# Two attention blocks on one core: weight stores and raw loads pinned in the transfer queue, normalising steps and chores at other places

## The chip, the cores and the metric

The kernel runs on one core of one Trainium2 chip. The metric is the device time in microseconds (us) of one execution; the number given for a kernel is the median of its runs. The core has five engines with a queue of instructions each: TensorE (PE, matrix products), VectorE (DVE) and ScalarE (ACT) for elementwise work, GpSimd (POOL) and SyncE (SP). Here SP issues the transfers (DMA) of weights, images and small exchanges, and POOL issues those that add one tile to another in flight. [...]

## What is computed

Two self-attention blocks one after the other, on 8 images of 512 channels and 32 x 32 positions (1024 positions), all in float32. Each block normalises its input in 8 groups of channels, makes queries, keys and values, attends in 8 heads of 64 channels, projects, and adds its input. The second block is the same with other weights. Cut to one block:

```python
xg = x.reshape(B, GROUPS, -1)
xn = ((xg - mean) * rsqrt(var + EPS)).reshape(B, C, H, W) * gamma + beta
qkv = einsum('oc,bchw->bohw', qkv_w, xn) + qkv_b
q, k, v = (B, 8 heads, 64, 1024 positions) each
attn = softmax(einsum('bhds,bhdt->bhst', q, k) * 64 ** -0.5, axis=-1)
out = einsum('bhst,bhdt->bhds', attn, v).reshape(B, C, H, W)
return x + einsum('oc,bchw->bohw', proj_w, out) + proj_b
```

## The kernel before

**Jobs.** One image in one layer is a job. The 16 jobs run in the order (image 0, layer 0), (1, 0), (0, 1), (1, 1), then the same for the next pair of images. Each job has a projection phase for V, for the output O of the job before, and for K and Q, and then an attention. The two phases alternate: while the attention of job n runs on TensorE, the other engines prepare the projections of job n+1.

**Projections.** The products are done with the seven products of Strassen's scheme, nested twice in the "deep" form (lines 801 and 806). Each weight therefore needs seven sums of its blocks, which are made once on VectorE and kept in DRAM. `factor` (lines 162 to 168) does one of four steps of such sums. Three helpers feed it: `load_blocks` (line 157) loads the four raw blocks, `store_factors` writes the sums of one level to DRAM (`keep`), and `deep_round` loads four blocks into a tile `round`, does both levels of sums on it, and stores the seven results (`deep`, line 235). `ROUNDS` says that jobs 0 to 3 each make one such round, in their attention; `FIRST` says that jobs 0 and 1 also make first-level sums (tile `raw`) there, through `put_first`. `prepare` makes the second-level sums of a first-level weight in place and stores them (line 209) after a delay given to `later`. `fetch` loads weights in advance into slots of the pool that also holds the exponentials e. The inputs of the deep form are sums too, of the normalised image: `combine` (lines 423 to 429) and `inner_sums` (lines 482 to 488, tile `deep`). The SBUF tiles named raw, round and deep share one tag, so they follow one another in the same place.

**Attention.** 64 steps per job, 8 groups of 8. A step makes scores of one block of keys against half of the queries (line 1099), ScalarE takes the exponential (line 1104), TensorE multiplies by V two steps later (line 1150). The row sums of the exponentials are added up beside this: in most groups the first four blocks are added in pairs by POOL's transfers (line 1127) and then to `acc` by VectorE (line 1130), the rest directly by VectorE (lines 1118 and 1120). At the end of a group ScalarE copies half of the result to `px` (line 1171) and VectorE adds the other half (line 1173). `reduce` makes the row sums of a group (line 1185); for every second group a chain follows that crosses the DMA queue twice: `r` is gathered by three transfers (line 1208), VectorE inverts (lines 1212 to 1232), the result `rt` goes to DRAM as `rd` (line 1225), comes back spread over partitions as `rb` in two transfers (line 1227), and VectorE multiplies (line 1242). In jobs with a round the first inversions are put off by 12.0 and the multiplication by 22.0 in planned time.

**What sets the order.** The program counts its own planned time: `advance` moves it by 1.71 per attention step, and `later(delay, fn)` puts a piece of work at a planned time. Chores of an attention are put at step numbers in two tables, `chores` (`put`) and `moves` (`move`); both step to the next free number when the wanted one is taken. Thus a table holds at most one chore per step, but the two may hold one each. The order on PE, ACT, DVE and POOL is the order of the program text. SP's instructions are ordered by a scheduler instead, from an estimate of when their inputs are ready, unless one is marked to stay in its place in the program: this is what `tc.keep_in_program_order` does.

The chores of an attention of job n, as far as they matter here: the normalisation of the next image is `reads` (statistics) and `steps`: one for the group sums, one for the factors (lines 349 to 351), and four `apply`, one ScalarE pass each (line 356); then the four `combine`, and the eight `inner_sums`, which `deep_steps` returns with those from xn first (line 482 `deep<-xn` first) and those from t after.

Of the kernel before, what the change touches and what calls it, by code (L numbers as in the profile page):

```python
# [19 lines left out]
P = 128  # L20
# [21 lines left out]
FACTOR = {1: A11, 2: A12, 3: S4, 4: A22, 5: S1, 6: S2, 7: S3}  # L42
# [12 lines left out]
ROUNDS = {0: (O, 0), 1: (V, 1), 2: (O, 1), 3: (V, 0)}  # L55
# [26 lines left out]
def fast_path(  # L82
# [10 lines left out]
    nc = tc.nc  # L93
# [18 lines left out]
    xs = {}  # L112
# [3 lines left out]
    def later(delay, fn):  # L116
        todo.append((clock[0] + delay, fn))
# [25 lines left out]
    def raw_block(layer, which, i, j):  # L143

        if which == O:
            w, at = wp[layer], 0
        else:
            w, at = wqkv[layer], {Q: 0, K: C, V: 2 * C}[which]
        cols = slice(at + i * CH, at + (i + 1) * CH)
        return w[j * CH : (j + 1) * CH, cols].rearrange("(cc p) o -> p cc o", p=P)  # L150

    factors, deep, begins = {}, {}, []

    def load_blocks(w, layer, which):
        for i in range(2):
            for j in range(2):
                nc.sync.dma_start(w[:, 2 * j + i], raw_block(layer, which, i, j))

    def factor(w, part):

        if part == 0:
            nc.vector.tensor_add(w[:, S1], w[:, S3], w[:, A22])
        elif part == 1:
            nc.vector.tensor_sub(w[:, S2], w[:, S1], w[:, A11])
        elif part == 2:
            nc.vector.tensor_sub(w[:, S3], w[:, A11], w[:, S3])
        else:
            nc.vector.tensor_sub(w[:, S4], w[:, A12], w[:, S2])

    def store_factors(w, layer, which):  # L170
        keep = wdram.tile([P, NW, 2, CH], F32, name=f"keep_{which}_{layer}")
        for s in (slice(S1, NW), slice(S3, S3 + 1)):
            nc.sync.dma_start(keep[:, s], w[:, s])
        factors[which, layer] = keep

    plan, held, raw = deque(), {}, set()
# [22 lines left out]
    def prepare(key):  # L199
        if key not in raw:  # L200
            return False
        raw.discard(key)
        n, which, o = key
        w = held[key]
        for part in range(4):
            factor(w, part)
        keep = wdram.tile([P, NW, P], F32, name=f"deep_{which}_{jobs[n][1]}_{o}")
        deep[which, jobs[n][1], o] = keep
        later(1.0, lambda: nc.sync.dma_start(keep, w))
        return True  # L210

    def deep_round(which, layer):


        box = []

        def start():
            t = acts.tile([P, NW, NW, P], F32, tag="deep", name=f"round_{which}_{layer}")
            box.append(t)
            for i in range(2):  # L220
                for j in range(2):
                    nc.sync.dma_start(
                        t[:, 2 * j + i, 0:4, :].rearrange("p (cc h) o -> p cc (h o)", cc=2),
                        raw_block(layer, which, i, j),
                    )

        def outer_(part):
            factor(box[0][:, :, 0:4, :], part)

        def inner(part):  # L230
            factor(box[0].rearrange("p f a o -> p a f o"), part)

        def store(o):
            keep = wdram.tile([P, NW, P], F32, name=f"deep_{which}_{layer}_{o}")
            nc.sync.dma_start(keep, box[0][:, FACTOR[o]])
            deep[which, layer, o] = keep

        first = [lambda part=part: outer_(part) for part in range(4)]
        second = [lambda part=part: inner(part) for part in range(4)]
        return start, first, second, [lambda o=o: store(o) for o in OUTER]  # L240
# [8 lines left out]
    def x_tile(b):  # L249
        xs[b] = xpool.tile([P, NC, S], F32, tag="x", name=f"x_{b}")  # L250
        return xs[b]
# [5 lines left out]
    def load_steps(b):  # L257

        def chunk(cc):
            if cc == 0:  # L260
                x_tile(b)
            nc.sync.dma_start(xs[b][:, cc, :], x[b, cc * P : (cc + 1) * P, :])

        return [(15 + cc, lambda cc=cc: chunk(cc)) for cc in range(NC)]

    class Norm:
# [20 lines left out]
        def sums(self, cc):  # L287

            nc.scalar.activation(
                xn[0][:, cc, :], xs[self.b][:, cc, :], AF.Identity, accum_out=self.mv[:, cc, 0:1]  # L290
            )
# [108 lines left out]
    def norm_steps(n):  # L400
        norm = Norm(n)

        def place():
            xn[0] = acts.tile([P, NC, S], F32, tag="xn", name=f"xn_{n}")

        def factors():
            norm.factors(slice(0, NC))
            place()

        reads = [lambda cc=cc, sh=sh: norm.stat(cc, sh) for cc in range(NC) for sh in range(2)]  # L410
        reads.append(norm.gather)
        steps = [norm.groups, factors] + [lambda cc=cc: norm.apply(cc) for cc in range(NC)]
        return reads, steps
# [220 lines left out]
    def deep_phases(n, extra, outs=None, early=()):  # L634
# [340 lines left out]
        for which, o in chains[:2]:  # L975
            prepare((job(which), which, o))
# [20 lines left out]
    def last_weights(n):  # L997
        w = acts.tile([P, NW, 2, CH], F32, tag="deep", name="w_last")
        layer = jobs[n][1]
        load_blocks(w, layer, O)  # L1000
        return w
# [341 lines left out]
    def extend_plan(n):  # L1343
        plan.extend((n, V, o) for o in (OUTER_V if n >= DEEP_V else ORDER))
        plan.extend((n - 1, O, o) for o in (OUTER if n >= DEEP_V else ORDER))
        plan.extend((n, which, o) for which in (K, Q) for o in OUTER)
# [192 lines left out]
    reads, steps = norm_steps(1)  # L1539
    for n in range(-1, len(jobs)):  # L1540
        last = n + 1 == len(jobs)
        outs = None
        if n >= 0:
            chores, moves = {}, {}

            def put(i, fn):
                while i in chores:
                    i += 1
                chores[i] = fn
                return i  # L1550

            def move(i, fn):
                while i in moves:
                    i += 1
                moves[i] = fn
                return i
# [12 lines left out]
                    at = move(at + 1 + i % 2, fn)  # L1569

            def put_first(which, layer):
                at = move(31 if n == 0 else 3, lambda: start()) + 3
                box = []

                def start():
                    box.append(acts.tile([P, NW, 2, CH], F32, tag="deep", name=f"raw_{n}"))
                    load_blocks(box[0], layer, which)

                for part in range(4):
                    at = put(at + 1, lambda part=part: factor(box[0], part))  # L1580
                move(at + 1, lambda: store_factors(box[0], layer, which))

            if last:
                w = last_weights(n)
                for part in range(4):
                    put(12 + 2 * part, lambda part=part: factor(w, part))
                for i, fn in enumerate(last_sums(0)):
                    put(49 + 3 * i, fn)
            else:
                for i, (_, fn) in enumerate(extra):  # L1590
                    put(2 + i, fn)
                if n == 1:
                    at = (8, 14, 15, 16, 18, 19, 21, 24, 27, 30)
                else:
                    for i, fn in zip((3, 3, 4, 5, 5, 6, 7, 7, 8), reads):
                        put(i, fn)
                    at = (16, 22, 23, 24, 26, 27, 29, 31, 33, 35)
                    if n < DEEP_V + 2:
                        at = (17, 23, 24, 25, 27, 28, 30, 32, 34, 36)
                for i, fn in zip(at, steps):  # L1600
                    put(i, fn)
                if n == 1:
                    put_first(*FIRST[n])
                if n in ROUNDS:
                    put_round(*ROUNDS[n])
                if n == 0:
                    put_first(*FIRST[n])
                for i, fn in zip(at[len(steps) :], sums(n + 1)):
                    put(i, fn)
                put(52 if n in ROUNDS else 48, lambda q=att.q: out_combine(q, None, 0))  # L1610
                deep_first = deep_steps(n + 1)
                if n + 1 >= DEEP_V:
                    for i, fn in enumerate(deep_first):
                        put(37 + 2 * i if n not in ROUNDS else (39, 40, 41, 43, 45, 47, 49, 50)[i], fn)
                else:
                    for at, fn in zip((46, 47, 48, 49), deep_first[4:]):
                        put(at, fn)
                move(58, lambda: extend_plan(n + 1))
                for _ in range(RING):
                    move(58, fetch)  # L1620
            assert max([*chores, *moves], default=0) < NT * len(att.groups) + LEAD
            if n + 1 >= DEEP_V and not last:
# [10 lines left out]
                if n + 2 < len(jobs):  # L1633
                    reads, steps = norm_steps(n + 2)
# [34 lines left out]
            if n + 2 < len(jobs):  # L1669
                reads, steps = norm_steps(n + 2)  # L1670
# [264 lines left out]
```

## Time and profile before

| what | us |
|---|---|
| median of 3 runs | 3175.92 (3175.18 to 3176.13) |
| the profiled execution | 3175.27 |
| its span, first to last instruction | 3173.5 |
| mean granted TensorE clock | 0.998 |
| ACT busy: exponentials, 1024 of 1025 ns | 1043.5 |
| PE busy: scores and values, 8192 matmuls each | 1058.3 and 1057.6 |
| DVE busy: accumulation (L1118, L1120, L1130) | 156.4, 389.7, 272.6 |

The profile's page gives each engine's busy time, the span in 40 slices, the DMA queues, the chain of work that ended last, and the costliest groups of instructions. Other views of the same trace give the instructions in order of time with the idle time before each and what ended it, or the busy time in chosen windows. The profiled time is 1.8 us longer than the span, and 0.65 us below the median. The DMA issues that matter here, from the page (queue, operation, count, size, and the median time from issue to landing):

```profile
w<-deep SPq DMA_DIRECT2D x399, 448.0 KB, 5.3
e<-e POOLq DMA_DIRECT2D x224, 512.0 KB, 4.7
...
rb<-rd SPq DMA_DIRECT2D x96, 256.0 KB, 3.9
...
deep<-w SPq DMA_DIRECT2D x28, 448.0 KB, 2.7
deep<-round SPq DMA_DIRECT2D x28, 448.0 KB, 4.4
```

### The profile page before, as it was taken

How to read it: one execution, taken by the hardware profiler on the slowest of the kernel's cores; microseconds unless marked ns; L12 is line 12 of the kernel's file. 1: busy time of each engine (PE TensorE's matmuls, PEld its weight loads, DVE VectorE, ACT ScalarE, POOL GpSimd, SP SyncE). 2: the span in 40 equal slices, each digit the busy share in tenths (PEclk: the TensorE clock that was granted, in tenths of full speed). 3: DMA queues.
4: the chain of work that ended last, by engine and by line, in shares of the span. 5: the costliest groups of instructions: out<-in, count | busy, mean ns of one | idle time of the engine just before them, and what ended most of it. 6: DMA issues, size and time to landing. Idle time of an engine off the chain costs nothing.

```text
span 3173.5 us, 62149 instructions
## 1 busy us (share of the span) xinstructions
PE 3153.8 (99%) x24093; PEld 1875.1 (59%) x24093; DVE 2635.5 (83%) x3571; ACT 2330.9 (73%) x4233; POOL 280.9 (9%) x318
## 2 busy tenths in 40 slices
PE   9999999999999999999999999999999999999999
PEld 7356384663846639366483754837557375573844
DVE  8797898978879788796978969789697887978967
ACT  5648687786877768777686776867768687686864
POOL 0100101001010010101001000010000100001000
PEclk9999999999999999999999999999999999999999
DMA  8546675565735455455554535446456463445733
GB/s 277 142 129 167 159 211 136 142 188 142 229 75 147 110 132 146 82 163 148 145 179 93 161 92 144 120 95 186 129 137 182 89 198 66 132 126 95 223 75 82
DMA packets 186190, 450.31 MB, mean 142 GB/s; under 512 B 37928, under 2 KB 54176, under 8 KB 185888
## 3 DMA queue, kind: packets, MB, share of 16 engines
q1 hardware_dynamic: 137040, 296.82, 27.7%
q0 software_dynamic: 48848, 149.44, 25.9%
q8 instruction: 192, 3.15, 0.4%
q14 instruction: 110, 0.90, 0.1%
HBM read 247.41 MB, written 48.17 MB: 93 GB/s over the span
## 4 chain that ended last, share of the span: by engine, by line
PE 90%; DVE 5%; DMA 2%; issue 1%; SPq 0%; ACT 0%; DVEq 0%; POOL 0%; ACTq 0%; POOLq 0%
PE sc L1099 24%; PE po L1150 24%; PE vd L806 11%; PE zd L806 11%; PE yd L806 5%; PE ud L806 4%; PE vd L801 4%; PE zd L801 3%; DVE acc L1120 1%; PE ud L801 1%; PE yd L801 1%; DMA rb<-rd 1%; PE z L553 1%; DMA rd<-rt 1%; DVE acc L1130 1%
## 5 line engine op out<-in xcount | busy, mean ns | idle before, releaser
L1104 ACT ACTIVATE e<-sc 128x1024 f32<-128x1024 f32 x1024 | 1043.5, 1025 | 575.1 <-PE sc L1099 546.9
L1099 PE MATMUL sc<-q,k 64*64 64x512 f32 x8192 | 1058.3, 589 | 2.8 <-ACT e L1104 2.8
L1150 PE MATMUL po<-e,v 64*64 64x512 f32 x8192 | 1057.6, 589 | 1.9 <-ACT e L1104 1.9
L1150 PEld LDWEIGHTS po<-e,v 64*64 64x64 f32 x8192 | 313.1, 133 | 567.9 <-issue 541.9
L1099 PEld LDWEIGHTS sc<-q,k 64*64 64x64 f32 x8192 | 310.9, 133 | 566.6 <-issue 506.0
L1120 DVE TENSOR_TENSOR acc<-acc,e 128x1024 f32<-128x1024 f32 x320 | 389.7, 1218 | 37.9 <-ACT e L1104 27.1
L1127 POOL DMA_DIRECT2D e<-e x224 | 192.8, 861 | 1758.7 <-ACT e L1104 1302.8
L1118 DVE TENSOR_TENSOR acc<-e,e 128x1024 f32<-128x1024 f32 x128 | 156.4, 1222 | 145.8 <-ACT e L1104 145.8
L1130 DVE TENSOR_TENSOR acc<-acc,e 128x1024 f32<-128x1024 f32 x224 | 272.6, 1217 | 1.7
L806 PE MATMUL zd<-deep,w 128*128 128x256 f32 x860 | 240.2, 379 | 1.0 <-ACT ud L501 1.0
L806 PE MATMUL vd<-deep,w 128*128 128x256 f32 x804 | 223.5, 379 | 0.0
L806 PEld LDWEIGHTS zd<-deep,w 128*128 128x128 f32 x860 | 163.3, 190 | 23.6 <-ACT ud L501 1.4
L806 PEld LDWEIGHTS vd<-deep,w 128*128 128x128 f32 x804 | 152.8, 190 | 20.8
L1185 DVE TRANSPOSE_TENSOR_REDUCE r<-acc 128x32 f32<-128x1024 f32 x128 | 159.4, 1245 | 4.3
L901 POOL DMA_DIRECT2D x<-p x61 | 72.9, 1195 | 972.3 <-ACT p L823 379.0
L848 DVE TENSOR_TENSOR p<-p,s 128x512 f32<-128x512 f32 x185 | 127.4, 689 | 20.5 <-ACT p L823 17.1
L801 PE MATMUL vd<-w,deep 128*128 128x128 f32 x840 | 119.3, 275 | 3.1 <-ACT ud L501 3.1
L848 DVE TENSOR_TENSOR q<-q,s 128x512 f32<-128x512 f32 x64 | 44.2, 690 | 87.0 <-ACT q L825 45.1
L801 PEld LDWEIGHTS vd<-w,deep 128*128 128x128 f32 x840 | 106.1, 192 | 3.6 <-ACT ud L501 3.6
L801 PE MATMUL zd<-w,deep 128*128 128x128 f32 x728 | 106.5, 275 | 0.3 <-ACT ud L501 0.3
L806 PE MATMUL vd<-os,w 128*128 128x256 f32 x364 | 105.5, 379 | 0.0
L1242 DVE TENSOR_TENSOR q<-q,rb 128x1024 f32<-128x1024 f32 x64 | 77.4, 1209 | 29.9 <-DMA rb<-rd 29.2
(296 smaller groups left out, 4849.7 us busy)
## 6 DMA issues: line engine op xcount, KB each, us to landing
w<-deep SPq DMA_DIRECT2D x399, 448.0 KB, 5.3
e<-e POOLq DMA_DIRECT2D x224, 512.0 KB, 4.7
x<-p POOLq DMA_DIRECT2D x61, 512.0 KB, 6.4
rb<-rd SPq DMA_DIRECT2D x96, 256.0 KB, 3.9
x<-x_dram SPq DMA_DIRECT2D x28, 512.0 KB, 4.1
out_dram<-x SPq DMA_DIRECT2D x28, 512.0 KB, 5.0
deep<-w SPq DMA_DIRECT2D x28, 448.0 KB, 2.7
deep<-round SPq DMA_DIRECT2D x28, 448.0 KB, 4.4
```

What stands on the lines that cost most here:

```text
L801: nc.tensor.matmul(ps[:, tokens], moving[i][:, tokens], lhs[:, FACTOR[i], :], start=(start and ti == 0), stop=True, skip_group_check=True,)
L806: nc.tensor.matmul(ps, lhs[:, FACTOR[i], :], moving[i], start=start, stop=True, skip_group_check=True,)
L848: nc.vector.tensor_add(to_, to_, five.to_broadcast([P, 2, QT]))
L1099: nc.tensor.matmul(sc[h * HD : (h + 1) * HD, j, :], k[r, hp, k0 : k0 + HD], q[r, hp, sh * HALF : (sh + 1) * HALF], start=True, stop=True,)
L1104: nc.scalar.activation(e, sc, AF.Exp, scale=SCALE)
L1118: nc.vector.tensor_add(acc[g], self.es[i - 1], e)
L1120: nc.vector.tensor_add(acc[g], acc[g], e)
L1127: nc.gpsimd.dma_start(self.summed[i], self.summed.pop(i - 1), accum_op=ALU.add)
L1130: nc.vector.tensor_add(self.acc[g], self.acc[g], self.summed.pop(i))
L1150: nc.tensor.matmul(po[g][j * HD : (j + 1) * HD, h, :], v[r, kc, d0 : d0 + HD], e[r, j, :], start=(kc == 0), stop=(kc == NT - 1),)
L1185: nc.vector.tensor_reduce(self.r[:, 0, m, :], self.acc.pop(g).rearrange("p j (b e) -> p (j b) e", e=RP), AX.X, ALU.add, apply_transpose=True,)
L1242: nc.vector.tensor_mul(place, place, box[0])
```

## The change

Six kinds of SP transfers are issued through a helper `in_turn` that marks them to stay in program order: the loads of raw blocks, the stores of first-level sums, the stores of second-level sums made by `prepare` (which also move from 1.0 to 3.0 after their place in planned time), the loads and stores of `deep_round`, and the later loads of images. The rest moves chores. In the attentions of jobs 0 to 3 the normalising steps after the first two go to the table `moves` and to other numbers; the `combine` steps are entered before those of the round and of `put_first`; `put_first` begins at 37 instead of 31 in job 0 and at 2 instead of 3 in job 1; the `inner_sums` of jobs 0, 2 and 3 take other numbers.

```diff
--- before.py
+++ after.py
@@ -151,10 +151,13 @@
 
     factors, deep, begins = {}, {}, []
 
+    def in_turn(to_, src):
+        tc.keep_in_program_order(nc.sync.dma_start(to_, src))
+
     def load_blocks(w, layer, which):
         for i in range(2):
             for j in range(2):
-                nc.sync.dma_start(w[:, 2 * j + i], raw_block(layer, which, i, j))
+                in_turn(w[:, 2 * j + i], raw_block(layer, which, i, j))
 
     def factor(w, part):
 
@@ -170,7 +173,7 @@
     def store_factors(w, layer, which):
         keep = wdram.tile([P, NW, 2, CH], F32, name=f"keep_{which}_{layer}")
         for s in (slice(S1, NW), slice(S3, S3 + 1)):
-            nc.sync.dma_start(keep[:, s], w[:, s])
+            in_turn(keep[:, s], w[:, s])
         factors[which, layer] = keep
 
     plan, held, raw = deque(), {}, set()
@@ -206,7 +209,7 @@
             factor(w, part)
         keep = wdram.tile([P, NW, P], F32, name=f"deep_{which}_{jobs[n][1]}_{o}")
         deep[which, jobs[n][1], o] = keep
-        later(1.0, lambda: nc.sync.dma_start(keep, w))
+        later(3.0, lambda: in_turn(keep, w))
         return True
 
     def deep_round(which, layer):
@@ -219,7 +222,7 @@
             box.append(t)
             for i in range(2):
                 for j in range(2):
-                    nc.sync.dma_start(
+                    in_turn(
                         t[:, 2 * j + i, 0:4, :].rearrange("p (cc h) o -> p cc (h o)", cc=2),
                         raw_block(layer, which, i, j),
                     )
@@ -232,7 +235,7 @@
 
         def store(o):
             keep = wdram.tile([P, NW, P], F32, name=f"deep_{which}_{layer}_{o}")
-            nc.sync.dma_start(keep, box[0][:, FACTOR[o]])
+            in_turn(keep, box[0][:, FACTOR[o]])
             deep[which, layer, o] = keep
 
         first = [lambda part=part: outer_(part) for part in range(4)]
@@ -259,7 +262,7 @@
         def chunk(cc):
             if cc == 0:
                 x_tile(b)
-            nc.sync.dma_start(xs[b][:, cc, :], x[b, cc * P : (cc + 1) * P, :])
+            in_turn(xs[b][:, cc, :], x[b, cc * P : (cc + 1) * P, :])
 
         return [(15 + cc, lambda cc=cc: chunk(cc)) for cc in range(NC)]
 
@@ -1569,7 +1572,7 @@
                     at = move(at + 1 + i % 2, fn)
 
             def put_first(which, layer):
-                at = move(31 if n == 0 else 3, lambda: start()) + 3
+                at = move(37 if n == 0 else 2, lambda: start()) + 3
                 box = []
 
                 def start():
@@ -1590,30 +1593,32 @@
                 for i, (_, fn) in enumerate(extra):
                     put(2 + i, fn)
                 if n == 1:
-                    at = (8, 14, 15, 16, 18, 19, 21, 24, 27, 30)
+                    at = (8, 14, 15, 16, 17, 18, 17, 19, 20, 21)
                 else:
                     for i, fn in zip((3, 3, 4, 5, 5, 6, 7, 7, 8), reads):
                         put(i, fn)
                     at = (16, 22, 23, 24, 26, 27, 29, 31, 33, 35)
                     if n < DEEP_V + 2:
-                        at = (17, 23, 24, 25, 27, 28, 30, 32, 34, 36)
-                for i, fn in zip(at, steps):
+                        at = (17, 24, 26, 27, 29, 30, 31, 32, 33, 34)
+                for i, fn in zip(at[:2], steps):
                     put(i, fn)
+                for i, fn in zip(at[2:], steps[2:]):
+                    move(i, fn)
                 if n == 1:
                     put_first(*FIRST[n])
+                for i, fn in zip(at[len(steps) :], sums(n + 1)):
+                    put(i, fn)
                 if n in ROUNDS:
                     put_round(*ROUNDS[n])
                 if n == 0:
                     put_first(*FIRST[n])
-                for i, fn in zip(at[len(steps) :], sums(n + 1)):
-                    put(i, fn)
                 put(52 if n in ROUNDS else 48, lambda q=att.q: out_combine(q, None, 0))
                 deep_first = deep_steps(n + 1)
                 if n + 1 >= DEEP_V:
                     for i, fn in enumerate(deep_first):
-                        put(37 + 2 * i if n not in ROUNDS else (39, 40, 41, 43, 45, 47, 49, 50)[i], fn)
+                        put(37 + 2 * i if n not in ROUNDS else ((39, 40, 41, 43, 45, 47, 49, 50) if n == 1 else (36, 37, 38, 40, 41, 43, 45, 47))[i], fn)
                 else:
-                    for at, fn in zip((46, 47, 48, 49), deep_first[4:]):
+                    for at, fn in zip((47, 48, 49, 50), deep_first[4:]):
                         put(at, fn)
                 move(58, lambda: extend_plan(n + 1))
                 for _ in range(RING):
```

The instructions stay the same in number on PE, ACT, DVE and POOL; PE's and POOL's order is the same. On ACT only the applies (L356) of jobs 0 to 3 change places. On SP there are six fewer in the listing, since neighbours group differently. In jobs 0, 2 and 3 the order of SP was, for group 1: the three of r, seven stores of round (in job 0 then the four loads of raw), rd, rb. It becomes: r, rd, rb twice, four stores of round, r of group 3, three stores of round (in job 0 then the four loads of raw, rd, rb of group 3, and the two stores of raw). In job 1 it was r, rd, rb, seven stores, r, and becomes r, rd, rb, three stores, r, four stores. In the start phase the stores of V's sums move behind the loads of K's weights. On DVE, in jobs 2 and 3, L423 moves behind L1242 and L427 ahead of the L1130 and L1185 of group 3, and L482 ahead of L1118 and two L1120 of group 4. In the program after, L482 waits for five semaphores in each of jobs 1 to 3, all of them of stores of round.

## The prediction

> **What bounds the kernel now.** I read the busy shares first, then what TensorE waited for, then short stretches of the timeline round each of those waits, and last the DMA queue. The page and the list of TensorE's waits:
>
> ```profile
> PE 3153.8 (99%) x24093; PEld 1875.1 (59%) x24093; DVE 2635.5 (83%) x3571; ACT 2330.9 (73%) x4233; POOL 280.9 (9%) x318
> ...
> PE vd L801 <- ACT ud L501: 3.1, 3, 1.1
> PE sc L1099 <- ACT e L1104: 2.8, 3, 1.7
> ```
>
> TensorE is the bound. The change removes none of its instructions, so all that can be won is idle time and half clock. Measured as start-to-start distances beyond the usual pitch, idle time sums to 13.6 us, to which one half-clock stretch is added. Most of it is in job 0, where one transfer starts a chain. The lines are of the timeline (start, duration, in brackets the idle time before and its releaser), the last is a row of the view by windows, whose PEclk is the third column from the end:
>
> ```profile
> 119.73 7.84 SPq L235 DMA_DIRECT2D deep<-round x7
> 132.33 3.10 SPq L157 DMA_DIRECT2D raw<-wqkv_dram  x4
> 135.47 0.98 SPq L1225 DMA_DIRECT2D rd<-rt  x1
> 141.84 0.64 SPq L1227 DMA_DIRECT2D rb<-rd  x1
> ...
> 149.04 1.23 DVE L1242 TENSOR_TENSOR q<-q,rb 128x1024 f32<-128x1024 f32 x1 [12.51 <-DMA rb<-rd]
> ...
> 153.84 1.09 PE L1099 MATMUL sc<-q,k 64*64 64x512 f32 x8 [1.71 <-ACT e L1104]
> ...
> 194.57 1.09 PE L1150 MATMUL po<-e,v 64*64 64x512 f32 x8 [1.88 <-ACT e L1104]
> ...
> 196.86 1.19 PE L553 MATMUL z<-w,xn 128*128 128x256 f32 x2 [1.21 <-DMA w<-wqkv_dram]
> ...
> 196.00:203.50 7.50, 6.64 (x17) 5.36 (x18) 7.15 (x7) 0.88 (x2) 0.00 (x0) 0.54 0.60 202
> ```
>
> rt was ready at 127.9, but its transfer went out at 135.47, behind seven stores and four loads in SP's queue. VectorE then stood 12.51 us at L1242, had no slack left to the end of the job (one gap of 1.58 us in 149 to 210), and arrived late: TensorE loses 1.89 (at 151.5), 2.05 (192.1) and 1.27 us (194.6), and the clock is half (0.54 in the window's column) for 6.83 us, which costs 3.08 us of TensorE's time.
>
> Jobs 1 to 3 show two small things: the normalising step put on both sides of a copy (one TensorE stall of 0.71 us each in jobs 2 and 3), and a late VectorE at the end of the attention, worth 1.06, 1.24 and 1.26 us.
>
> ```profile
> 529.56 0.57 ACT L1171 COPY px<-po 128x512 f32<-128x512 f32 x1
> 530.03 1.25 ACT L356 ACTIVATE xn<-x,off,mul 128x1024 f32<-128x1024 f32 x1
> ...
> 532.25 1.09 PE L1099 MATMUL sc<-q,k 64*64 64x512 f32 x8 [0.53 <-ACT e L1104]
> ...
> 544.08 1.23 DVE L1242 TENSOR_TENSOR q<-q,rb 128x1024 f32<-128x1024 f32 x1 [3.17 <-DMA rb<-rd]
> ...
> 557.80 1.22 DVE L482 TENSOR_TENSOR deep<-xn 128x1024 f32<-128x1024 f32 x1
> ```
>
> [...] rd landed 6.4 us after its issue behind the stores (135.47 to 141.84), and had waited 7.6 us before that. [...] The trace has 6.83 us at half clock[...], after idle times of 1.9 and 1.2 us with slow work between.
>
> **The change part by part.**
>
> *Job 0's round stores.* SP's order becomes r, rd, rb, rb, four stores, r of the next group, three stores, four loads. rd goes out at 127.9. Its landing takes between 1.8 us (as unloaded elsewhere) and 6.4; then rb takes the page's median 3.9: it is there by 134 to 138. L1242 then follows work that ends at 135.4 (L423 moves behind it), so at most 2.6 of the 12.51 us remain. New waits: the factor steps of raw need its loads, which stand behind r of group 3 and three stores (0 to 2 us), and L482 for t needs both stores of raw (estimated 2.8 us). VectorE's end, 5.6 us late before, is then some 2 us late, about what jobs 2 and 3 show with their 1.2 us stalls. I count all of 1.89, 2.05 and the half clock 3.08, with 1.7 from the 1.27 and the 0.585 that follow it at 204.96: 8.7 us gained. Should the waits be longer, 196.86 remains late and the half clock with it: 4 gained.
>
> *Normalising steps apart (L356).* ScalarE needs 0.92 us for an exponential (two in 1.94) and 1.15 for an apply (527.51 to 528.66) against 1.716 per step; with the px copy (some 0.5) elsewhere, it falls back about 0.35 us per apply, twice in a row at most 0.8, inside the slack of some 1.5 us. Gain 2 × 0.71 = 1.4; bounds 0 and 1.4.
>
> *The new wait, jobs 1 to 3.* The L482 step writes a buffer that takes the place of round's, so it waits for all of round's stores. Before, they had been issued long ahead (those of job 2 at 526.89, L482 at 557.80). Now three of them (four in job 1) are tied behind r of group 3, which waits for VectorE's L1185. What is queued behind L482 on VectorE is the whole accumulation, with no idle time to the end: in job 2 after 544.08 its gaps sum to 0.15 us, in job 1 there is one of 2.17, in job 3 one of 2.21, and these two move along since their rd hangs on a step behind L482. So VectorE is later by the new wait less the old waits that go.
> Job 2: the rb wait of 3.17 goes and L423 (1.14) moves behind: L1242 at 539.8; from there to the end of L1185 7.69 plus L423 and L427 (2.25): 549.7. r's three issues take 2.44: 552.15. Three stores: last issue after 2 × 0.43 (the shortest L235 row) to 2 × 1.04, landing 2.7 (median of deep<-w) to 4.4 (deep<-round) later: 555.7 to 558.6. L482 gets there at 550.8: it waits 4.9 to 7.8, net 1.7 to 4.6.
> Job 3, same sum from 737.7 with r at 3.01: waits 5.4 to 8.4, less the 2.38 that goes: 3.0 to 6.0.
> Job 1: r issued from 354.61 to 357.70, four stores: 361.7 to 365.4 against 358.27: 3.4 to 7.1; nothing goes.
> r's issues themselves took 1.84 in other places (157, 118), so 3 × about 0.6 to 1.2 may come off: sums 5.1, 8.1 and 17.7. Each late microsecond at the end is TensorE's, as before's lateness of 1.36 and stall of 1.24 in job 2 show. I take 6.6, near the cheap end, because SP's queue is nearly empty at r, and rank it above zero because L482's list of semaphores in the new order names the stores behind r. Bounds: −3.6 (no new wait, and the 1.06, 1.24 and 1.26 go too) and 17.7.
>
> *Start phase.* Stores of V's factors (1 MB) now go after the K loads, weight loads ahead of deep stores. TensorE's stall of 1.14 us at 72.90 is a late weight; its load moves ahead of one store. I take 0.6 gained, bounds −1.5 to 1.1.
>
> *All else at nothing.* Deep stores 3.0 after their factors instead of 1.0 (the first goes out at 37.7, the first load of deep at 202.5); image loads (512 KB, 4.1 us to land) are used steps later; the DVE swaps keep the sum of work. Their cover is the job's length; gone, one load would cost its 4 us once.
>
> Sum against the profiled run's 3175.27 us (span 3173.5 and 1.8 around it; the median is 0.65 above): −8.7 − 1.4 − 0.6 + 6.6 = −4.1, so 3171.2, say 3171.
>
> **Rivals.**
> - *The L482 waits don't come or are absorbed* (stores land while r is in flight, or the end has slack I don't see). For: three stores are only 1.3 MB. Against: the order of SP. −8.7 − 1.4 − 0.6 − 3.6 = −14.3: 3161; half absorbed 3166.
> - *Slower, by half clock at the starts of jobs 2, 3 and 4.* The waits at mid price (11.4) make TensorE stand about 4 to 5 us in one piece three times; [...] the clock drops, as at 196, at 3.08 each. −10.7 + 11.4 + 9.2 = +9.9: 3185; at full price with one such drop +10.1 as well. [...] For: job 0's drop came with even shorter stops. Against: the stops now are 1.1 to 1.3 and my own price for the waits is below this.
> - *Job 0's chain doesn't break*: rb still late[...]. Then only 0 to 4 of the 8.7 comes: 3176 to 3180.
>
> **How the numbers follow.** My case 0.50 (3166 to 3176), no wait 0.22, half clock 0.18, job 0 unchanged 0.10. A measurement of this kernel can tell about 0.2%, 6.3 us: faster means below 3169.6, slower above 3182.3. Of my case 0.17 lies below 3169.6 and 0.33 between; with 0.22 and with job 0's 0.07 and 0.03, faster is 0.39, same 0.40, slower 0.21. The range 3163 to 3183 leaves out about 0.05 below and 0.14 above. My case's own range is 3166 to 3176.
>
> **What would show it.** L1242 at about 136 with no long wait before it, and no stall at 153.8 and 194.6; clock whole at 196. In jobs 2 and 3, no stall beside L356. VectorE's L482 with idle time of 4 to 8 us before it, released by deep<-round, three times, and stops at the job ends (L801, ACT ud) of 2 to 5 us instead of 1.1 to 1.3. I am wrong if L482 shows no wait, or if job ends don't grow with it, or if the clock falls at a job's start.

## The result and the profile after

| | us |
|---|---|
| before, median of 15 runs | 3176.13 (3172.44 to 3180.26) |
| changed, median of 15 runs | 3183.83 (3181.10 to 3186.80) |
| ratio changed / before | 1.0023, 95% interval 1.0015 to 1.0031 |
| span of the profiled execution | 3181.6 (before 3173.5) |

The changed kernel is slower by 0.23%, some 7.7 us. Line numbers beyond L154 are 3 higher in the changed kernel than in the one before (L482 is L485, L1242 is L1245); in some experiments they are 2 higher again. Every transfer issued through `in_turn` has that helper's line, L155. The list of what TensorE waited for in the changed kernel (line waited for: total us, times, longest):

```profile
PE vd L804 <- DMA w<-deep: 9.2, 4, 4.0
PE v L556 <- DVE q L1176: 3.0, 1, 3.0
PE z L556 <- DMA w<-wqkv_dram: 1.7, 1, 1.7
```

The two waits for an exponential that stood near the head of the list before (2.8 and 1.9 us) are gone. In their place stands a wait for the first weights of a projection phase, which before came to 0.2 us.

The way to find where 8 us of 3180 went is to compare the start of the same TensorE instruction in both traces, since TensorE does the same instructions in the same order. The table gives how much each stage became longer than in the kernel before, for all runs of this study (us; a negative number is a gain). Job ends include the projection phase that follows. Each row is one profiled execution. Before 20 us the profiled executions differ in their half clock (6.83 us of it from 8.50 in the kernel before, none in the changed one), so this column tells nothing.

```
stage (us of before)  to 20  to 100 | job 0  | job 1: first  end  | job 2: first  end  | job 3: first  end  | rest    sum
                                    100-300    300-330   330-500    500-560   560-700    700-735   735-1000
changed               -0.40  -1.21    -2.15     +0.74     +4.52      -0.76     +3.62      -0.76     +3.52     +0.57   +7.69
e1_untie_round        +0.16  -1.24    +7.76     +0.73     +2.21      -0.76     +0.92      -0.76     +0.26     +0.27   +9.55
e2_tie_job0           -0.58  -1.25    -1.42     +0.73     +1.65      -0.76     +0.89      -0.76     -0.05     +0.43   -1.12
e3_stores_early       -1.60  -1.25    -5.13     +0.73     +2.54      -0.76     +1.75      -0.76     +1.36     +0.26   -2.85
e4_deep_late          -1.54  -1.25    -2.31     +0.73     +3.46      -0.76     +0.06      -0.76     +0.86     +0.26   -1.25
f1_all_ahead          -1.56  -1.25    -5.28     +0.73     +2.57      -0.76     -1.61      -0.76     -1.79     +0.26   -9.45
f2_best               +0.09  -0.26    -5.59     +0.00     +2.52      -0.76     -0.78      -0.76     -1.20     +0.27   -6.46
f3_apply_apart        -0.91  +3.10    -1.76     +0.00     +3.50      -0.76     +3.67      -0.76     +3.89     +0.26  +10.22
f4_free_first_level   -0.50  -1.25    -1.17     +0.73     +2.64      -0.76     +3.84      -0.76     +3.44     -0.01   +6.20
g1_ahead_and_apart    -0.38  -1.14    -3.53     +0.00     +2.55      -0.76     -1.21      -0.76     -1.80     +0.25   -6.79
g2_free_old_job0      -1.00  -1.25    +4.62     +0.73     +0.93      -0.76     +1.00      -0.76     +0.01     -0.02   +3.49
g3_old_job1           -1.62  -0.78    -5.16     +0.00     +0.05      -0.76     -1.61      -0.76     -1.87     +0.27  -12.24
```

In the changed kernel the ends of jobs 1 to 3 cost 11.66 us (4.52 + 3.62 + 3.52), and job 0 gives only 2.15.

**Job 0.** The timeline of the changed kernel, lines of SP, VectorE and TensorE:

```profile
125.83 0.33 SPq L1228 DMA_DIRECT2D rd<-rt  x1
127.22 1.31 SPq L1230 DMA_DIRECT2D rb<-rd  x2
128.57 5.22 SPq L155 DMA_DIRECT2D deep<-round  x4
...
134.51 1.23 DVE L1245 TENSOR_TENSOR q<-q,rb 128x1024 f32<-128x1024 f32 x1 [1.16 <-DMA rb<-rd]
...
154.03 1.92 SPq L155 DMA_DIRECT2D raw<-wqkv_dram  x4
...
162.25 0.69 DVE L165 TENSOR_TENSOR raw<-raw 128x512 f32<-128x512 f32 x1 [6.33 <-DMA raw<-wqkv_dram]
...
200.05 1.99 PE L556 MATMUL v<-w,t 128*128 128x256 f32 x8 [2.98 <-DVE q L1176]
...
239.56 0.70 PE L809 MATMUL zd<-os,w 128*128 128x256 f32 x2 [1.69 <-ACT yd L500]
```

rd goes out as soon as rt is there, and the 12.51 us of waiting at the multiplication are 1.16. But there is a new wait. The tile raw takes the place of round, and its loads wait until round's stores have landed. Three of these stores, issued from 147.16 to 149.16, now stand behind r of group 3 (144.45), and SP waits 4.7 us in two pieces for stores of round. The loads go out at 154.03, and VectorE stands 6.33 us for them; before the change it didn't wait there. TensorE has won 6.7 us in this job when it comes to the product `v<-w,t` of the next projection at 200.05. Then it loses 2.6 us there, waiting for VectorE, and 1.9 at 239.56, where ScalarE has stood 2.64 us for a transfer of p (0.29 before). So the phase after the attention takes back 4.4 of the 6.7 us.

**Job ends 1 to 3.** For jobs 1 and 3, SP's lines and VectorE's step that makes the first sum of the deep form:

```profile
353.33 1.84 SPq L1211 DMA_DIRECT2D r<-r  x3
355.21 2.88 SPq L155 DMA_DIRECT2D deep<-round  x4
...
361.58 1.23 DVE L485 TENSOR_TENSOR deep<-xn 128x1024 f32<-128x1024 f32 x1 [4.51 <-DMA deep<-round]
...
752.23 3.42 SPq L1211 DMA_DIRECT2D r<-r  x3
755.68 1.72 SPq L155 DMA_DIRECT2D deep<-round  x3
...
760.77 1.23 DVE L485 TENSOR_TENSOR deep<-xn 128x1024 f32<-128x1024 f32 x1 [7.46 <-DMA deep<-round]
```

r goes when VectorE has reduced group 3 (L1188 ends at 353.31 and 752.20), and three or four stores stand behind it. L485 writes where round lay and waits 4.51 and 7.46 us for them; in job 2 it is idle 6.94 us at the same place (the view names no releaser there). How this reaches TensorE shows in the timeline at the end of job 3:

```profile
793.96 1.30 SPq L1230 DMA_DIRECT2D rb<-rd  x2
795.42 6.97 SPq L192 DMA_DIRECT2D w<-deep  x7
801.83 0.68 PE L804 MATMUL vd<-w,xn 128*128 128x128 f32 x4 [3.96 <-DMA w<-deep]
```

and for the clock in the view by windows at the end of job 1 (window, its length, busy time of PE, PEld, DVE, ACT and POOL, PEclk, DMA share, GB/s):

```profile
398.70:402.10 3.40, 3.29 (x18) 3.11 (x19) 3.19 (x3) 1.60 (x5) 0.00 (x0) 0.64 1.03 409
```

The weights of the next phase are issued right behind rb, and rb hangs on VectorE's inversion. With VectorE late, the first weight is late, TensorE stands 3.96 us (3.17 in job 1), and after both stops the clock is half for 3.41 us (from 802.40, and from 399.63 in job 1). The delay grows by another 1.4 us there (1.8 in job 1).

### The profile page after: what moved, and what is told of

Its sections match the earlier page's. It is cut to its first block, busy times and chain, and to the rows that moved or that the text cites. A ratio compares the mean times of both kernels' runs of the same rounds, so it can differ in the third digit from the quotient of the medians.

```text
span 3181.6 us, 62172 instructions
## 1 busy us (share of the span) xinstructions
PE 3154.0 (99%) x24093; PEld 1875.9 (59%) x24093; DVE 2636.2 (83%) x3571; ACT 2332.2 (73%) x4233; POOL 281.0 (9%) x318
## 4 chain that ended last, share of the span: by engine, by line
PE 94%; DVE 2%; DMA 2%; issue 1%; ACT 1%; SPq 0%; DVEq 0%; ACTq 0%
PE sc L1102 26%; PE po L1153 26%; PE vd L809 11%; PE zd L809 11%; PE yd L809 5%; PE ud L809 4%; PE vd L804 4%; PE zd L804 3%; PE ud L804 1%; PE yd L804 1%; PE z L556 1%; DVE acc L1123 1%; DMA w<-deep 1%; DMA x<-p 0%; ACT e L1107 0%
## 5 line engine op out<-in xcount | busy, mean ns | idle before, releaser
L1130 POOL DMA_DIRECT2D e<-e x224 | 192.9, 861 | 1756.6 <-ACT e L1107 1362.1
L1188 DVE TRANSPOSE_TENSOR_REDUCE r<-acc 128x32 f32<-128x1024 f32 x128 | 159.4, 1245 | 4.3
L809 PE MATMUL zd<-os,w 128*128 128x256 f32 x356 | 99.0, 379 | 1.7 <-ACT yd L500 1.7
```

What stands on the lines that cost most here:

```text
L809: nc.tensor.matmul(ps, lhs[:, FACTOR[i], :], moving[i], start=start, stop=True, skip_group_check=True,)
L1130: nc.gpsimd.dma_start(self.summed[i], self.summed.pop(i - 1), accum_op=ALU.add)
L1188: nc.vector.tensor_reduce(self.r[:, 0, m, :], self.acc.pop(g).rearrange("p j (b e) -> p (j b) e", e=RP), AX.X, ALU.add, apply_transpose=True,)
```

## The experiments

Theory A: the stores of the round held behind r make L485 wait, and this makes the ends of jobs 1 to 3 late; the same hold, in job 0, puts rd ahead and brings the gain. Theory B: the new places of the chores on VectorE and ScalarE cost the time, wherever the stores are. "Held" means marked to stay in program order, "free" means ordered by the scheduler. Each ratio is to runs of the kernel before on the same chip.

**The round's stores free again** (e1_untie_round), and **held in job 0 alone** (e2_tie_job0):

```diff
 # e1_untie_round
-            in_turn(keep, box[0][:, FACTOR[o]])
+            nc.sync.dma_start(keep, box[0][:, FACTOR[o]])
 # e2_tie_job0
+            (in_turn if (which, layer) == ROUNDS[0] else nc.sync.dma_start)(
+                keep, box[0][:, FACTOR[o]]
+            )
```

> The changed kernel with one thing undone: the seven stores of each round are no longer held in program order (everything else of the change stays). In the listing they then go out in one block, in jobs 0, 2 and 3 ahead of rd, in job 1 ahead of r. Theory A (the stores held behind r of group 3 make L485 wait, and with it the job ends 1 to 3 late; the same hold gave job 0 its gain): the waits of 4.5, 6.9 and 7.5 us at L485 are gone, jobs 1 to 3 cost at most 1 us against the kernel before instead of some 11.8, but job 0 is as before: the wait for rb at L1245 is back at 10 to 12 us, its 8.3 us of gain and the 4.4 lost right after both go; total 3172 to 3177. Theory B (the new places of the chores on VectorE and ScalarE cost the time, whatever the stores do): job ends 1 to 3 stay as late as in the changed kernel, and with job 0's gain gone the total is 3186 to 3192.

> The changed kernel with the stores of the round held in program order in job 0 only; those of jobs 1 to 3 are free, as in the kernel before. Theory A: job 0 keeps its gain of 8.3 us (and the 4.4 us lost just after it), L485 waits for no store of jobs 1 to 3, and jobs 1 to 3 together cost between 1 us less and 1 us more than before: total 3170 to 3174, 10 to 13 us under the changed kernel. Theory B: the three job ends still cost some 12 us, total 3181 to 3185.

e1: 3185.0 us, ratio to before 1.0029 (1.0018 to 1.0040). e2: 3174.85 us, 0.9995 (0.9986 to 1.0003). In both, the waits at L485 are gone in jobs 2 and 3, and 2.10 and 2.18 us are left in job 1. The three job ends cost 3.39 us in e1 and 2.49 in e2, where the changed kernel has 11.66. So about 8 to 9 us of those are the hold, as theory A says; some 2 remain in job 1, which A had not expected and which puts e2 just above its range (g3 below takes this up). Where A was clearly wrong is job 0 without the hold: it isn't as before, but 7.76 us worse, and e1's total misses A's range by 8 us. VectorE's line of e1:

```profile
148.79 1.23 DVE L1245 TENSOR_TENSOR q<-q,rb 128x1024 f32<-128x1024 f32 x1 [14.92 <-DMA rb<-rd]
```

It waits longer than the 12.51 before, because L426 (L423 before), which used to stand ahead of it, now stands behind. The new places in job 0 are thus good only with the hold; this is followed up in g2.

**Fewer stores behind r** (e3_stores_early: none in job 0, three in job 1, one in jobs 2 and 3; f1_all_ahead: none in jobs 0, 2 and 3, one in job 1), in two lines of the placing of the round:

```diff
-                at = max(at + 3, 25)
+                at = max(at + 3, 23)      # f1_all_ahead: max(at + 1, 22)
                 for i, fn in enumerate(stores):
-                    at = move(at + 1 + i % 2, fn)
+                    at = move(at + 1, fn)
```

> The changed kernel with the stores of the round put at earlier, consecutive places (from 23 instead of 25, without the free places between); still held in order. In the listing one store goes ahead of rd and six after rb and ahead of r of group 3 in job 0 (all seven ahead of r), six ahead of r and one behind in jobs 2 and 3; in job 1 it stays at three ahead and four behind. Theory A, if what counts is how many stores stand behind r: one store is issued 0.9 us sooner than three, so the waits at L485 in jobs 2 and 3 shorten only from 6.9 and 7.5 to 5.5 to 6.5, and job 1 keeps 4.5: total 3180 to 3184. If instead the data of three stores make up the wait, it falls to about 3 in jobs 2 and 3 and the total to 3175 to 3178. Theory B: no change from 3183.8 within 1 us.

> The changed kernel with the stores of the round at 22 and on, consecutive, still held in order: in the listing all seven go ahead of r of group 3 in jobs 0, 2 and 3 (two of them ahead of rd), six of seven in job 1. The sums of the deep form keep the early places. Theory A (only the stores behind r make L485 wait): no wait for a store in jobs 2 and 3, so those two job ends cost what they did with the stores free (0.9 and 0.0 us against before, where the changed kernel has 3.6 and 3.5), job 1 about 1 us less than the 4.5 of the changed kernel; the two stores ahead of rd bring the wait for rb back to 2 to 5 us. Total 3172 to 3176. Theory B (the early places of L485 cost by themselves): job ends 2 and 3 keep 2 us or more each without any wait at L485.

e3: 3175.07 us, 0.9994 (0.9985 to 1.0002). f1: 3167.32 us, 0.9974 (0.9963 to 0.9985). In job 2, first e3, then f1, both from the timeline:

```profile
545.07 2.68 SPq L1211 DMA_DIRECT2D r<-r  x3
547.79 0.58 SPq L155 DMA_DIRECT2D deep<-round  x1
...
551.10 1.22 DVE L485 TENSOR_TENSOR deep<-xn 128x1024 f32<-128x1024 f32 x1 [4.96 <-DMA r<-r]
```

```profile
529.17 6.20 SPq L155 DMA_DIRECT2D deep<-round  x5
545.31 2.88 SPq L1211 DMA_DIRECT2D r<-r  x3
546.31 1.22 DVE L485 TENSOR_TENSOR deep<-xn 128x1024 f32<-128x1024 f32 x1
```

One store behind r still costs a wait of 4.96 us (5.37 in job 3), mostly r's own issue (2.68 us in job 2) and one landing (2.73 from the end of the store's issue to L485); with none behind r there is no wait in jobs 2 and 3. With 3, 1 and 0 stores behind r the ends of job 2 cost 3.62, 1.75 and -1.61 us, of job 3 3.52, 1.36 and -1.79: a clean series, and against theory B, since L485 stands at its new place in all three. (e1 has none behind r either, and ends of +0.92 and +0.26; there the free stores go ahead of rd, and VectorE waits 5.42 and 5.40 us for rb.) In job 1 the number behind r makes no difference: with three in e3 and one in f1, L485 waits 3.30 and 3.13 us.

The numbers expected for the totals were too pessimistic: I had left the gain of job 0 at 2 us, but with the stores ahead of r it is 5.1 to 5.3. The traces show where it comes from. In e3 raw's loads go out at 146.07 instead of 154.03, and VectorE waits 0.56 us for them instead of 6.33. It is so in all traces with the hold in job 0: 0.54 to 0.56 us in the five with all stores ahead of r (e3, f1, f2, g1, g3), 6.33 to 6.98 in the five with three behind (the changed kernel, e2, e4, f3, f4). No run moves raw's loads alone. The wait for rb in f1 did not come back to 2 to 5 us either, but was 1.42 and 1.52 in jobs 2 and 3.

**The deep sums back at their old places** (e4_deep_late), the stores still held:

```diff
-((39, 40, 41, 43, 45, 47, 49, 50) if n == 1 else (36, 37, 38, 40, 41, 43, 45, 47))[i]
+((39, 40, 41, 43, 45, 47, 49, 50) if n == 1 else (39, 40, 41, 43, 45, 47, 49, 50))[i]
```

> The changed kernel with the eight sums of the deep form (L485 and on) at the places of the kernel before in jobs 0, 2 and 3 (from 39 instead of 36); the stores keep their order. L485 is then asked for three attention steps later, after L1121 and two L1123 of group 4 (3.5 us of work). Theory A: the waits of L485 in jobs 2 and 3 shrink by 3 to 3.5 us each, job 1 stays; the two job ends come 3 us earlier each: total 3176 to 3180. Theory B, that the earlier places themselves do harm or good without the wait: within 1 us of 3183.8 unless the other chores pushed aside cost more.

3177.22 us, 1.0001 (0.9993 to 1.0010), as expected. In job 2:

```profile
556.85 1.22 DVE L485 TENSOR_TENSOR deep<-xn 128x1024 f32<-128x1024 f32 x1 [3.12 <-DMA deep<-round]
```

The wait is 3.12 us here and 3.63 in job 3, each 3.8 less than in the changed kernel, and the two ends cost 0.06 and 0.86 instead of 3.62 and 3.52. With work of group 4 ahead of it, L485 is asked for later, while the stores land as they did. So the hold makes the wait and the earlier place lengthens it: putting the stores ahead of r removes it in jobs 2 and 3, the later place halves it. Job 1, unchanged here, waits 4.51 us and loses 3.46.

**A first combination** (f2_best): stores as in f1 with job 1's free, deep sums late, job 1's normalising apart.

```diff
-            in_turn(keep, box[0][:, FACTOR[o]])
+            (nc.sync.dma_start if (which, layer) == ROUNDS[1] else in_turn)(
+                keep, box[0][:, FACTOR[o]]
+            )
-                    at = (8, 14, 15, 16, 17, 18, 17, 19, 20, 21)
+                    at = (8, 14, 15, 16, 18, 20, 21, 22, 23, 24)
...
```

> A combination meant to be fast: the changed kernel with the stores of the round consecutive from 22 (job 1's left free), the sums of the deep form at the places of the kernel before, and the four normalising passes of job 1 at 15, 16, 18 and 20 with its combine steps from 21. Theory A: job 0 gains 4 to 6 us net, job 1 loses at most 1, jobs 2 and 3 within 0.5 of before or up to 1.5 below, the 0.73 us lost at job 1's normalising is gone: total 3166 to 3171, below the kernel before by 0.15 to 0.3 per cent. Theory B: no better than 3175.

3169.01 us, 0.9978 (0.9970 to 0.9987), as expected; but the ends of jobs 2 and 3 gain less than in f1 (-0.78 and -1.20 against -1.61 and -1.79), and job 1 loses 2.52 at its end, not the 1 at most that I expected. By g1 below, which differs from f2 in this alone, the earlier places of the deep sums are worth 0.4 and 0.6 us once the stores are out of the way. That is little more than the spread: f1, g1 and g3 have the same edits in job 2, and its end is -1.61, -1.21 and -1.61.

**Job 1's normalising and the start** (f3_apply_apart, f4_free_first_level):

```diff
 # f3_apply_apart
-                    at = (8, 14, 15, 16, 17, 18, 17, 19, 20, 21)
+                    at = (8, 14, 15, 16, 18, 20, 21, 22, 23, 24)
-        later(3.0, lambda: in_turn(keep, w))
+        later(1.0, lambda: in_turn(keep, w))
 # f4_free_first_level
-            in_turn(keep[:, s], w[:, s])
+            nc.sync.dma_start(keep[:, s], w[:, s])
```

> The changed kernel with two edits in places that don't touch: the normalising passes of job 1 at 15, 16, 18, 20 instead of 15 to 18 (combine steps after them), and the stores of prepare at 1.0 instead of 3.0. If four passes in four neighbouring steps overrun ScalarE (each 0.35 us more than a step), the 0.73 us lost there goes; if the stall is from VectorE it stays. The start phase, 1.2 us better than before in the changed kernel at 74 us, stays better if the order of the stores of first-level sums makes it, and falls back if the delay of prepare's stores does. Everything after job 1's first half as in the changed kernel: total 3182 to 3184.

> The changed kernel with the stores of first-level sums free again (in the start phase the listing then has V's first stores ahead of K's last weight loads, as before). If their order makes the start phase's 1.2 us, it goes; if not, it stays. Job 0's tie of the raw stores goes too: L485 for t may wait up to 1 us less there. Jobs 1 to 3 as in the changed kernel: total 3183 to 3186.

f3: 3185.89 us, 1.0027 (1.0016 to 1.0039). f4: 3182.50 us, 1.0018 (1.0010 to 1.0026). They lie 1.9 us above and 0.5 below what was expected. The 0.73 us lost in job 1's first half is ScalarE's: in f3, and in every run with the passes apart, it is 0.00. ScalarE in the changed kernel:

```profile
312.96 1.23 ACT L359 ACTIVATE xn<-x,off,mul 128x1024 f32<-128x1024 f32 x1
314.09 1.01 ACT L1107 ACTIVATE e<-sc 128x1024 f32<-128x1024 f32 x1
314.99 0.58 ACT L1174 COPY px<-po 128x512 f32<-128x512 f32 x1
315.46 1.25 ACT L359 ACTIVATE xn<-x,off,mul 128x1024 f32<-128x1024 f32 x1
```

From 310.91 to 318.64 it does four passes, three exponentials and a px copy, 7.73 us, in which TensorE at 1.716 us a step would use up 4.5 exponentials. The start phase's 1.2 us stays with the first-level stores free (f4: -1.25) and is gone, with 3.1 lost, when prepare's stores go early (f3). That speaks for the delay of 3.0; but f2, g1 and g3, which have this delay and the same edits there as the changed kernel, show -0.26, -1.14 and -0.78, and f3's loss contains a half-clock stretch at 75.6. One execution each: it stays open.

**What is left of jobs 1 and 0** (g1_ahead_and_apart: f2 with the deep sums at the early places; g3_old_job1: g1 with all chores of job 1 as before; g2_free_old_job0: e1 with all chores of job 0 as before):

```diff
 # g3_old_job1 against g1_ahead_and_apart
-                    at = (8, 14, 15, 16, 18, 20, 21, 22, 23, 24)
+                    at = (8, 14, 15, 16, 18, 19, 21, 24, 27, 30)
-                    move(i, fn)
+                    (put if n == 1 else move)(i, fn)
...
-                at = move(37 if n == 0 else 2, lambda: start()) + 3
+                at = move(37 if n == 0 else 3, lambda: start()) + 3
 # and for n == 1 the combine steps are entered after put_round again
```

> The stores of the round all ahead of r (consecutive from 22, job 1's left free), the deep sums at the early places, and job 1's normalising passes apart. Theory A, from the stages measured so far: job 0 about 5.3 us better than before, nothing lost at job 1's normalising, about 2 lost at its end, jobs 2 and 3 each 0.8 better in the first half and 1.6 to 1.8 at the end: 9 to 10 us under before, 3165 to 3168. If the gain at the ends of jobs 2 and 3 was luck of one execution, 3168 to 3171.

> Stores all ahead of r as in the run with all seven ahead, deep sums at the early places, job 1's stores free and its chores at the places of the kernel before. In job 1 some 2.5 us were lost even without a wait at L485. If the new places of job 1's chores cause it, job 1's end is back within 0.7 of before and the total is 3164 to 3167; if it is VectorE, which has no idle time left there and cannot follow a TensorE that comes 5 us earlier, 2 us or more stay: total 3165.5 to 3169.

> The changed kernel with the stores of the round free and, in job 0 alone, every chore at its place in the kernel before. VectorE's order in job 0 is then that of the kernel before, as is SP's. If the loss of 7.8 us in job 0 with free stores comes from the new places of the chores (work moved behind a multiplication that then waits 15 us for rb), job 0 is back within 1.5 us of before and the total is 3176 to 3179; if it comes from the ties of raw's loads and stores, job 0 keeps 5 us or more and the total is 3182 to 3186.

g1: 3167.96 us, 0.9974 (0.9962 to 0.9985), as expected. The gains at the ends of jobs 2 and 3 are there again (-1.21 and -1.80); job 0 has 1.7 us less than in f1, and its trace has a half-clock stretch at 236.6.

g3: 3163.43 us, 0.9962 (0.9948 to 0.9976), the fastest of all, and just below what was expected. The end of job 1 costs 0.05 us instead of 2.55. VectorE's lack of slack was the other explanation, and it isn't what decides: job 0's gain is as large (-5.16), and job 1 follows. So the new places of job 1's chores cost 2.5 us. But they do it by a wait, not by themselves as theory B has it: my expectation said that L485 doesn't wait in job 1 when the stores are free, and the traces show that it does. First g1, then g3 (L487 is the step of L485, L238 stores round):

```profile
341.25 6.50 SPq L238 DMA_DIRECT2D deep<-round  x7
...
357.81 1.23 DVE L487 TENSOR_TENSOR deep<-xn 128x1024 f32<-128x1024 f32 x1 [3.24 <-DMA deep<-round]
```

```profile
335.06 6.97 SPq L238 DMA_DIRECT2D deep<-round  x7
...
351.18 1.22 DVE L487 TENSOR_TENSOR deep<-xn 128x1024 f32<-128x1024 f32 x1
```

The four combine steps, 1.2 us each, stand among the round's eight steps in g1, as in the changed kernel, and behind them in g3. So VectorE ends the round at 341.22 in g1 and at 333.65 in g3; 2.5 us of this were there when the job began. The stores can go only then, and the first sum of the deep form meets them. No run takes away this wait alone, so its share of the 2.5 us is not measured.

g2: 3180.89 us, 1.0015 (1.0008 to 1.0021), between the two expectations. Job 0 costs 4.62 instead of 7.76: 3.1 us were the chores' places. Of the rest a part may be the ties of raw, since VectorE waits 3.79 us at L485 for the stores of raw, which it did not before; and the clock is half for 10.24 us in this job, where the kernel before has 6.83. No run separates the two.

## Why the prediction was wrong

The terms of its sum beside what they measured:

| term | predicted | measured |
|---|---|---|
| job 0 with the phase after it | -8.7 | -2.15 |
| applies of jobs 2 and 3 | -1.4 | -1.52 |
| new wait at the ends of jobs 1 to 3 | +6.6 | +11.66 |
| start phase | -0.6 | -1.21 |
| applies of job 1, tail of the job list | 0 | +0.74, +0.57 |
| sum, with -0.40 before 20 us | -4.1 | +7.69 |

The applies came as predicted. The start phase gained 1.21, just above its bound of 1.1, and what makes it stays open. Two large terms failed.

*Job 0.* The first half held word for word: rd goes out at once, L1245 waits 1.16 us, the two stalls are gone and the clock is whole at 196. Two steps then failed. The first is the price of the new wait for raw's loads, "0 to 2 us": it is 6.33. I had counted r and three stores ahead of the loads, but not that raw takes round's place, so that SP waits once more until those stores have landed. The trace before showed this pause in the lines of the prediction: the stores are issued by 127.57, the loads go out at 132.33. VectorE, which I had some 2 us late at its end, is then late enough for TensorE to wait 1.70 us for a weight and 2.98 for VectorE's addition. With the wait at 0.54, in f1 and g3, job 0 gains 5.3 and 5.2 of the 8.7. The second step is that I took the phase after it as free. In f1 and g3 8.5 of the 8.7 are won, and then TensorE loses 0.8 us at `v<-w,t` and 2.3 to 2.5 behind the transfer of p, for which the sum had nothing. A stall that goes is worth only what the next resource allows.

*The wait at L485.* It is there in all three jobs, for the reason given: 4.5, 6.9 and 7.5 us, inside the bounds of 3.4 to 7.1, 4.9 to 7.8 and 5.4 to 8.4. The step that failed is the choice of 6.6 near the cheap end "because SP's queue is nearly empty at r": r's three issues took 1.84 us only in job 1, and 2.66 and 3.42 in jobs 2 and 3, where the waits lie above the middle of their bounds. Two smaller steps failed with it. The rb waits of 3.17 and 2.38 did not go, but became 1.08 and 1.26, and job 1 got a new one of 1.59; VectorE's idle time in these stretches thus grew by 17.3 us in all, close to the bound of 17.7. And not every late microsecond of VectorE is TensorE's: the ends cost 11.66, of which some 3 are the half clock at the starts of jobs 2 and 4. The half clock was priced, but only in the rival, to which I gave a chance of 0.18.

*The rival that came nearest.* Stops at the ends of the jobs with the clock falling after them are what happened, at two of the three starts. That it said 3185, and 3183.8 was measured, is in good part luck: it priced the ends with the half clock at 20.6 us, where they cost 11.66, and took job 0's 8.7 as won. The two stops, of 3.17 and 3.96 us, are also shorter than the 4 to 5 us that it counted on.

*What I hadn't seen.* The prediction called the DVE swaps free since they keep the sum of work. In job 1 they cost 2.5 us (g1 against g3), since the combine steps make the round and its stores late. And it took the applies of jobs 0, 2 and 3 into account, not the four of job 1 in neighbouring steps.

The rival that job 0's chain doesn't break is refuted by the timeline, though its number for the job (0 to 4 of the 8.7) was met in another way; that the waits don't come, by the three waits of L485.

## What to carry to other kernels

Holding a transfer in program order fixes what it stands behind as well as what it is ahead of: place it ahead of the next instruction that waits for a slow engine, here ahead of r, and check who reuses the buffer that it reads: here both the next writer on VectorE and the next loads stood for it. With this one shift the same change is 0.26% faster than before instead of 0.23% slower, and 0.38% faster when the second job's chores are left alone and its stores free. When a new order costs time though it keeps the sum of work, look for the transfer that it makes late. When a stall is removed, price the next stage at the earlier arrival, not at its old slack; and when a term has bounds, take the cheap end only for a reason that the trace shows in that place.

## What the runs showed of the hardware

The half clock came in stretches of 3.41 us (from 399.63 and 802.40 in the changed kernel) or twice that (6.83, from 196.23 in the kernel before). In the changed kernel the clock fell after stops of TensorE of 3.17 and 3.96 us (starts of jobs 2 and 4), but stayed whole after one of 2.98 us that ended at 200.05; before the change it fell after two short ones of 1.88 and 1.21. The length of one stop didn't decide alone.

What else went with it can be read from the same two traces. Their half-clock stretches begin a whole number of 3.413 us apart: 118 times in the changed kernel (399.63 and 802.40), 55 times in the one before (8.50 and 196.23). Counted in lengths of 3.413 us from these starts, TensorE was busy for 1.09 us of the length just before the fall at 196.23, and for 0.98 and 0.57 us of those before 399.63 and 802.40. Between 20 us and the last 10 us, the least that it was busy in a length at full clock without a fall behind it is 1.70 us in the kernel before (from 151.86) and 1.61 in the changed one (from 198.24). In the first 20 us, though, the fall at 8.50 came after a length with 2.16 us.

The stop of 2.98 us is cut by the border between two such lengths at 198.24: TensorE is busy for 2.24 us of the one and 1.61 of the other, and the clock stays whole. So where a stop lies seems to count beside how long it is. This rests on three falls in traces taken for other questions; no run was made to test it.
